# One of two graph product banks of the third slot is taken from the values: what a shift in a rotation of PSUM banks does

## Chip, cores, metric

One core of one Trainium2 chip. The metric is the device time of one execution in microseconds (us), median of several runs; each change is compared with runs of the kernel before on the same chip. Ratios are the mean time of one kernel's fast runs over that of the other's of the same rounds, so not quite the ratio of the medians quoted beside them. All runs told here were of the fast state. Names in the profile: PE is the TensorE's matmul, PEld its weight load, DVE the VectorE, ACT the ScalarE, POOL the GpSimd, SP the SyncE, which issues transfers. PSUM is the memory in which the kernel keeps PE's products, in banks.

## The reference, cut to what matters

64 graphs of 256 nodes with 512 features, fp32. A graph layer, then attention with 8 heads over the same mask, each with a residual and a layer norm:

```python
x = layernorm(x + gnn(x, adj, W, b))          # deg*(x Wi' + b) + A x Wj'
q, k, v = x Wq' + bq, x Wk' + bk, x Wv' + bv   # 8 heads of 64
out = softmax(mask(q k' / 8)) v
x = layernorm(x + out Wo' + bo)
```

## The kernel before

The kernel works on pairs of graphs; in one loop body it finishes the attention of one pair and does the graph layer of the next. Its matrix products are cut into seven block products (a Strassen scheme), whose left operands are sums of blocks. In the profile each fp32 matmul of the program stands as two pieces (a product of four matmuls is a row of x8); the graph products, whose operands are cast to fp32r, stand as one each, four to a product.

The kernel shares out eight banks of PSUM. Two score tiles hold two banks each, the values of the attention have one, and three go round among everything else:

```python
ps_s = ...(name="ps_s", bufs=2, space=PSUM)   # scores: 2 x 2 banks
ps_v = ...(name="ps_v", bufs=1, space=PSUM)   # values: 1 bank
ps_m = ...(name="ps_m", bufs=3, space=PSUM)   # all other products: 3 banks

def bank(name):
    return ps_m.tile([P, 512], F32, tag="mm", name=name)

def score_banks(name):
    return ps_s.tile([P, 2, 512], F32, tag="sc", name=name)
```

The graph stage makes, for each quarter c of the features, one product in a bank (`pa`), which ACT copies out and DVE reads in four sums:

```python
def take_input(b, c, pa):
    nc.scalar.copy(xl[b][:, c]..., pa[:, :3 * P])
    ...
    nc.vector.tensor_add(f["S1"][:, c], a21, f["A22"][:, c])
    nc.vector.tensor_sub(f["S3"][:, c], f["A11"][:, c], a21)
    nc.vector.tensor_sub(f["S2"][:, c], a22, f["S3"][:, c])
    nc.vector.tensor_sub(f["S4"][:, c], a12, f["S2"][:, c])   # last reader of the bank

def l0_inputs(b, half, borrow=False):
    ...
    for c in (2 * half, 2 * half + 1):
        pa = score_banks("pa")[:, 0, :] if borrow else bank("pa")
        ...                                                   # four matmuls
        take_input(b, c, pa)
```

The order of the work in a loop body (four slots between the products of the attention; b1, b2 are the graphs of the next pair, p and q their seven graph layer products, o the seven of the output projection):

```python
return [[item(l0_inputs, b1, 0, True), item(l0_inputs, b1, 1)],
        p[0:3] + [item(split_x, b2)] + p[3:4],
        p[4:7] + [item(l0_inputs, b2, 0)],
        [item(l0_inputs, b2, 1), q[0], q[1], item(h_transpose, b1, 1, True),   # third slot
         q[2], item(h_transpose, b1, 0, True)],
        q[3:], ...]
...
# fourth slot
run(o[:1] + rest[:1] + o[1:2] + rest[1:2])
combine_left(oS[g], in_order)
end_values(inverses)
run(rest[2:] + o[2:5] + work[SLOTS + 1] + o[5:6] + work[SLOTS + 2] + o[6:])
```

In the third slot pa2 and pa3 stand for the two graph products of `l0_inputs(b2, 1)`, x for product q[0] (it reads A11), w for q[1] (A22), A12 for q[2], which adds to x. In the profile `po` is the bank of such a product, `pav` that of the values, `den` that of the softmax sums.

Of the kernel before, what the change touches and what calls it, by code (L numbers as in the profile page):

```python
# [8 lines left out]
F32 = mybir.dt.float32  # L9
# [7 lines left out]
P = 128  # L17
# [208 lines left out]
def unshifted_path(ctx, tc, flag, x, adj, wiT, wjT, b0, wqT, bq, wkT, bk, wvT, bv, woT, bo, out):  # L226
# [14 lines left out]
    B, N, D = x.shape  # L241
# [21 lines left out]
    ps_v = ctx.enter_context(tc.tile_pool(name="ps_v", bufs=1, space=PSUM))  # L263
    ps_m = ctx.enter_context(tc.tile_pool(name="ps_m", bufs=3, space=PSUM))

    def bank(name):
        return ps_m.tile([P, 512], F32, tag="mm", name=name)

    def score_banks(name):
        return ps_s.tile([P, 2, 512], F32, tag="sc", name=name)  # L270


    def in_order(ins):

        tc.keep_in_program_order(ins)
# [4 lines left out]
    def matmul(*args, **kw):  # L280
        in_order(nc.tensor.matmul(*args, **kw))  # L281
# [194 lines left out]
    def input_tiles(b):  # L476
        xl[b] = p2.tile([P, NC, 3, P], F32, tag="xl", name="xl")
        a11, a12, a22 = (xl[b][:, :, m, :] for m in range(3))
        xS[b] = left_blocks(a11, a12, None, a22, p2.tile([P, 4, NC, P], F32, tag="xS", name="xS"))

    def graph_product(b, c, pa, n, t, part):
        matmul(pa[:, t * P:(t + 3) * P], part[:, t, c * P:(c + 1) * P], graph[:, t, :],
               start=(n == 0), stop=(n == 2 * NT - 1), skip_group_check=True)

    def take_input(b, c, pa):
        nc.scalar.copy(xl[b][:, c].rearrange("p m n -> p (m n)"), pa[:, :3 * P])
        _, a12, a22, a21 = (pa[:, m * P:(m + 1) * P] for m in range(4))
        f = xS[b]
        nc.vector.tensor_add(f["S1"][:, c], a21, f["A22"][:, c])
        nc.vector.tensor_sub(f["S3"][:, c], f["A11"][:, c], a21)  # L490
        nc.vector.tensor_sub(f["S2"][:, c], a22, f["S3"][:, c])
        nc.vector.tensor_sub(f["S4"][:, c], a12, f["S2"][:, c])  # L492

    def l0_inputs(b, half, borrow=False):


        if half == 0:
            input_tiles(b)
        for c in (2 * half, 2 * half + 1):
            pa = score_banks("pa")[:, 0, :] if borrow else bank("pa")  # L500
            for n, (t, part) in enumerate((t, part) for t in range(NT) for part in (xhi[b], xlo[b])):
                graph_product(b, c, pa, n, t, part)
            take_input(b, c, pa)
# [12 lines left out]
    def l0_steps(b):  # L516
        banks = {}

        def product(name, lname, n, first):
            if first:  # L520
                banks[name] = bank("po")[:, :H]
            for c in range(NC):
                matmul(banks[name], xS[b][lname][:, c, :], w0[:, n, c, :], start=(first and c == 0),
                                 stop=(c == NC - 1), skip_group_check=True)

        def place(t, j):
            return xh[b][:, t, j * H:(j + 1) * H]

        def add_to(dst, src):
            nc.vector.tensor_add(dst, src, dst)  # L530

        def step1():
            product("x", "A11", B11, True)
            u1 = p2.tile([P, H], F32, tag="lu", name="u1")
            nc.scalar.copy(u1, banks["x"])

            rest = xh[b].rearrange("p t (j o) -> p (t j) o", j=2)[:, 1:]
            nc.gpsimd.tensor_tensor(rest, rest, u1.unsqueeze(1).to_broadcast([P, 3, H]), ALU.add)  # L538

        def step2():  # L540
            product("w", "A22", T4, True)
            add_to(place(1, 0), banks["w"])

        def step3():
            product("x", "A12", B21, False)
            add_to(place(0, 0), banks["x"])

        def step4():
            product("y", "S2", T2, True)
            add_to(place(0, 1), banks["y"])  # L550

        def step5():
            product("z", "S1", T1, True)
            add_to(place(1, 1), banks["z"])

        def step6():
            product("y", "S3", T3, False)
            h = xh[b][:, 1, :].rearrange("p (j o) -> p j o", j=2)
            add_to(h, banks["y"].unsqueeze(1).to_broadcast([P, 2, H]))
            norm(xh[b][:, 1, :])  # L560

        def step7():
            product("z", "S4", B22, False)
            add_to(place(0, 1), banks["z"])
            norm(xh[b][:, 0, :])

        return [step1, step2, step3, step4, step5, step6, step7]
# [19 lines left out]
    def pair_blocks(m, tag):  # L587

        s = p1.tile([P, 4, 2, N], F32, tag=tag, name=tag)
        return left_blocks(m[:, 0:2, 0:N], m[:, 2:4, 0:N], m[:, 0:2, N:2 * N], m[:, 2:4, N:2 * N], s)  # L590
# [60 lines left out]
    def qk_steps(g, store, tag, bias, diff):  # L651

        def new_store():
            store[g] = p1.tile([P, NC, NB * N], F32, tag=tag, name=tag)

        def place(i, j):
            return store[g][:, 2 * j:2 * j + 2, i * N:(i + 1) * N]

        def biased(b):
            def evict(dst, ps):  # L660
                for m in range(2):
                    nc.scalar.activation(dst[:, m, :], ps[:, m, :], AF.Identity, bias=b[:, m:m + 1], scale=1.0)
            return evict

        def last(dst, ps, addend):
            for m in range(2):
                nc.vector.scalar_tensor_tensor(dst[:, m, :], ps[:, m, :], diff[:, m:m + 1],  # L667
                                               addend[:, m, :], ALU.add, ALU.add)

        return qkv_steps(g, True, new_store, place, biased(bias), biased(diff), last)  # L670
# [98 lines left out]
    pavs = {}  # L769
# [7 lines left out]
    def values(g, w):  # L777
        i, pr = divmod(w, NC)
        if w == 0:
            aoT[g] = p1.tile([P, NC, NB * N], F32, tag="aoT", name="aoT")  # L780
            oS[g] = pair_blocks(aoT[g], "oS")
        pp = w % 2
        if pp == 0:
            pavs[g] = ps_v.tile([P, 2, N], F32, tag="av", name="pav")
        pe, _ = made[g, w]
        for kc in range(NT):
            for j in range(2):
                h0 = (2 * pr + j) * DH
                matmul(pavs[g][j * DH:(j + 1) * DH, pp, :], vv[g][:, i, kc, h0:h0 + DH], pe[:, j, kc, :],
                       start=(kc == 0), stop=(kc == NT - 1))  # L790
# [55 lines left out]
    def layer0(g):  # L846

        b1, b2 = NB * g, NB * g + 1

        def item(f, *args):  # L850
            return lambda: f(*args)

        p, q = l0_steps(b1), l0_steps(b2)
        return [[item(l0_inputs, b1, 0, True), item(l0_inputs, b1, 1)],
                p[0:3] + [item(split_x, b2)] + p[3:4],
                p[4:7] + [item(l0_inputs, b2, 0)],
                [item(l0_inputs, b2, 1), q[0], q[1], item(h_transpose, b1, 1, True),
                 q[2], item(h_transpose, b1, 0, True)],
                q[3:],
                [item(h_transpose, b2, 1, True)], [item(h_transpose, b2, 0, True)]]  # L860

    def run(steps):
        for s in steps:
            s()
# [17 lines left out]
    p, q = l0_steps(0), l0_steps(1)  # L882
# [3 lines left out]
    bias_steps()  # L886
    make_factors(wqT, "wq", raw_q)
    run(p[5:])
    l0_inputs(1, 0, True)
    l0_inputs(1, 1)  # L890
    make_factors(wkT, "wk", raw_k)
    for _ in range(AHEAD):
# [7 lines left out]
    q = qk_steps(0, qT, "qT", bq_sb, bqd)  # L900
# [18 lines left out]
    for g in range(NG - 1):  # L919
        load_x(NB * (g + 2))  # L920
        load_x(NB * (g + 2) + 1)
        work = layer0(g + 1)
        run(work[0])
        for w in range(2, NB * NC, 2):
            values(g, w - 2)
            values(g, w - 1)
            multiply()
            divide_two(g, w - 1)
            later = [scores(g, w), scores(g, w + 1)]
            part = work[w // 2]  # L930
            n = 0 if w == NB * NC - 2 else 1
            run(later[:n] + part[:1] + later[n:] + part[1:])
        w = NB * NC - 2
        values(g, w)
        values(g, w + 1)
        multiply()
# [8 lines left out]
        q = qk_steps(g + 1, qT, "qT", bq_sb, bqd)  # L945
# [10 lines left out]
    g = NG - 1  # L956
# [89 lines left out]
```

## Time and profile before

| | before |
|---|---|
| median of the first 3 runs | 3230.88 us (3230.29 to 3233.19) |
| PE busy | 3189.2 us, 99% of the span |
| next engine, DVE | 59% |
| granted PE clock | 0.998 |
| one period of the loop | 99.68 us, 31 of them |

How to read it: PE is the bound, by its busy share, but "busy" has modelled ends in it: pieces that start 216 ns apart are drawn 380 ns long. What PE loses is read from the distance between starts of matmuls, as the prediction does. The period is taken from the first graph product of one loop body to that of the next; 31 bodies give 30 such distances.

### The profile page before, as it was taken

Reading aid. Unit: us, or ns where it says so; the run is one execution under the profiler, and the core shown is the slowest. Engines: PE = TensorE matmul, PEld = TensorE weight load, DVE = VectorE, ACT = ScalarE, POOL = GpSimd, SP = SyncE. Lnnn points to the kernel's source line nnn. Section 1 sums busy time; section 2 is a strip of 40 time slices with the busy share of each in tenths; the row PEclk is TensorE's granted clock in tenths of the full one; section 3 lists DMA queues with packets and bytes.
Section 4 is the critical chain, followed back from the end, with each engine's and each line's share of the span. In section 5 each row is a group of like instructions: output and inputs, shape, how many; then the busy total and the mean of one; then the engine's idle time right before and its main releaser. Section 6 shows DMA issues by size and latency. Waiting matters only on the chain. (4 is left out here: it accounts for less than half of the span.)

```text
span 3230.8 us, 48219 instructions
## 1 busy us (share of the span) xinstructions
PE 3189.2 (99%) x17398; PEld 2617.4 (81%) x17398; DVE 1892.0 (59%) x3847; ACT 1113.0 (34%) x2146; POOL 1506.9 (47%) x1191
## 2 busy tenths in 40 slices
PE   8999999999999999999999999999999999999998
PEld 6888888888888888888888888888888888888885
DVE  6655556555565555655556655556555565555665
ACT  2333333333333333333333333333333333333333
POOL 3454444544445444455444454344544445444443
PEclk9999999999999999999999999999999999999999
DMA  7234432344323433223443234432334322444223
GB/s 246 64 107 122 121 97 74 102 118 123 112 66 92 120 121 118 74 87 111 123 123 90 74 106 121 121 106 67 99 119 123 113 69 90 118 121 119 80 70 92
DMA packets 257168, 340.90 MB, mean 106 GB/s; under 512 B 29856, under 2 KB 154272, under 8 KB 256928
## 3 DMA queue, kind: packets, MB, share of 16 engines
q1 hardware_dynamic: 256928, 337.76, 34.9%
q8 instruction: 143, 2.34, 0.3%
q14 instruction: 97, 0.79, 0.1%
HBM read 274.73 MB, written 37.75 MB: 97 GB/s over the span
## 5 line engine op out<-in xcount | busy, mean ns | idle before, releaser
L454 POOL TENSOR_TENSOR rstd<-ve,mhalf 128x1 f32<-128x1 f32 x256 | 140.6, 549 | 813.6 <-DVE below L452 813.0
L281 PE MATMUL po<-w,xS 128*128 128x256 f32 x2048 | 474.9, 382 | 4.4 <-DVE xh L530 0.5
L281 PE MATMUL st<-hS,factor 128*128 128x256 f32 x2048 | 454.4, 380 | 2.5 <-DVE u L636 2.5
L763 POOL TENSOR_TENSOR pk<-pe 128x512 f32<-128x512 f32 x256 | 322.1, 1274 | 276.9 <-ACT pe L760 276.9
L281 PEld LDWEIGHTS po<-w,xS 128*128 128x128 f32 x2048 | 384.4, 190 | 77.4 <-DVE xh L530 17.2
L281 PEld LDWEIGHTS st<-hS,factor 128*128 128x128 f32 x2048 | 390.2, 191 | 56.3 <-DVE u L636 2.9
L281 PE MATMUL po<-w,xl 128*128 128x256 f32 x1536 | 360.1, 384 | 16.8 <-DVE xS L492 15.9
L760 ACT ACTIVATE pe<-pe 128x1024 f32<-128x1024 f32 x256 | 270.2, 1057 | 248.2 <-DVE pe L756 248.2
L281 PEld LDWEIGHTS po<-w,xl 128*128 128x128 f32 x1536 | 284.0, 190 | 73.3 <-PE po L281 22.9
L281 PE MATMUL st<-hT,factor 128*128 128x256 f32 x1536 | 342.2, 379 | 1.0 <-DVE qT L667 1.0
L636 DVE TENSOR_TENSOR u<-st,u 128x512 f32<-128x512 f32 x96 | 66.4, 692 | 468.8 <-PE st L281 461.6
L756 DVE TENSOR_TENSOR pe<-ps,maskT 128x1024 f32<-128x1024 f32 x256 | 297.1, 1201 | 67.6 <-PE ps L281 67.6
L530 DVE TENSOR_TENSOR xh<-po,xh 128x256 f32<-128x256 f32 (+1 forms) x384 | 170.5, 458 | 268.2 <-POOL xh L538 197.1
L281 PEld LDWEIGHTS st<-hT,factor 128*128 128x128 f32 x1536 | 291.7, 190 | 40.9 <-DVE qT L667 1.4
L281 PE MATMUL ps<-qT,kT 64*128 64x256 f32 x2048 | 256.5, 389 | 0.0
L281 PE MATMUL pav<-pe,v_sb 128*64 128x256 f32 x2048 | 250.1, 386 | 1.9 <-ACT pe L760 1.8
L281 PEld LDWEIGHTS ps<-qT,kT 64*128 64x128 f32 x2048 | 187.0, 186 | 68.2 <-issue 51.3
L281 PE MATMUL st<-factor,hS 128*128 128x256 f32 x1024 | 234.8, 382 | 0.0
L281 PE MATMUL st<-factor,oS 128*128 128x256 f32 x992 | 229.4, 379 | 0.0
L833 DVE RECIPROCAL rden<-den 128x256 f32<-128x256 f32 x96 | 168.8, 1758 | 91.6 <-PE den L281 86.1
L281 PEld LDWEIGHTS st<-factor,hS 128*128 128x128 f32 x1024 | 191.9, 190 | 35.4 <-issue 10.6
L459 ACT ACTIVATE shift<-below,rstd 128x1 f32<-128x1 f32 x256 | 75.4, 294 | 415.2 <-POOL rstd L454 409.6
(112 smaller groups left out, 5035.9 us busy)
## 6 DMA issues: line engine op xcount, KB each, us to landing
xh<-in_x_dram SPq DMA_DIRECT2D x64, 512.0 KB, 4.0
factor<-wq SPq DMA_DIRECT2D x128, 256.0 KB, 2.7
factor<-wk SPq DMA_DIRECT2D x128, 256.0 KB, 2.6
factor<-wv SPq DMA_DIRECT2D x128, 256.0 KB, 4.3
factor<-wo SPq DMA_DIRECT2D x124, 256.0 KB, 2.7
out_dram<-xh SPq DMA_DIRECT2D x62, 512.0 KB, 4.1
factor<-in_wqT_dram SPq DMA_DIRECT2D x96, 256.0 KB, 2.7
factor<-in_wkT_dram SPq DMA_DIRECT2D x96, 256.0 KB, 2.7
```

The source lines that it names most:

```text
L281: in_order(nc.tensor.matmul(*args, **kw))
L454: nc.gpsimd.tensor_tensor(rstd, ve, mhalf, ALU.pow)
L459: order(nc.scalar.activation(shift, below, AF.Identity, scale=rstd))
L530: nc.vector.tensor_add(dst, src, dst)
L636: nc.vector.tensor_add(new("u2"), bank["y"], k["u1"])
L756: nc.vector.tensor_add(pe.rearrange("p j t q -> p j (t q)"), ps.rearrange("p j t q -> p j (t q)"), maskT.rearrange("p t q -> p (t q)").uns ...
L760: in_order(nc.scalar.activation(flat, flat, AF.Exp, scale=QSCALE, accum_out=etot[:, NB * g + i, pr:pr + 1]))
L763: nc.gpsimd.tensor_tensor(pk, pe[:, :, 0, :], pe[:, :, 1, :], ALU.add)
L833: nc.vector.reciprocal(rden, den)
```

## The change

Intent: in the third slot the first graph product goes to the bank of the values, which is free there, so that one tile fewer goes round the three banks and w gets the bank of another, earlier tile.

```diff
+    def score_bank(name):
+        return score_banks(name)[:, 0, :]
+
+    def value_bank(name):
+        return ps_v.tile([P, 512], F32, tag="av", name=name)
...
-    def l0_inputs(b, half, borrow=False):
+    def l0_inputs(b, half, borrow=()):
...
-            pa = score_banks("pa")[:, 0, :] if borrow else bank("pa")
+            pa = borrow[c % 2]("pa") if borrow else bank("pa")
...
-            pavs[g] = ps_v.tile([P, 2, N], F32, tag="av", name="pav")
+            pavs[g] = value_bank("pav").rearrange("p (r q) -> p r q", r=2)
...
-        return [[item(l0_inputs, b1, 0, True), item(l0_inputs, b1, 1)],
+        return [[item(l0_inputs, b1, 0, (score_bank, score_bank)), item(l0_inputs, b1, 1)],
...
-                [item(l0_inputs, b2, 1), q[0], q[1], item(h_transpose, b1, 1, True),
+                [item(l0_inputs, b2, 1, (value_bank, bank)), q[0], q[1], item(h_transpose, b1, 1, True),
```

(One more call, ahead of the loop, gets its argument in the new form.)

## The prediction

> **What bounds the kernel now.** I read the page's head first, then the waits of PE, then one period of the loop in order of time, on PE and on the engines that free its banks.

> ```profile
> span 3230.8 us, 48219 instructions
> PE 3189.2 (99%) x17398; PEld 2617.4 (81%) x17398; DVE 1892.0 (59%) x3847; ACT 1113.0 (34%) x2146; POOL 1506.9 (47%) x1191
> PEclk9999999999999999999999999999999999999999
> ```

> PE is busy 3189.2 of 3230.8 us at a full clock, no other engine over 59%. So the end is set by PE, and a change that neither removes matmuls nor makes them shorter can win at most PE's lost time. The program has 17398 matmuls before and after; what order each engine gets is the same too (I compared the built programs: only waits differ). The waits of PE say where it is lost:

> ```profile
> PE po L281 <- DVE xS L492: 15.9, 32, 4.5
> PE pt_a L284 <- DVE a L324: 4.1, 1, 4.1
> PE st L281 <- DVE u L636: 2.5, 1, 2.5
> PE pa L281 <- ACT xhi L368: 2.2, 1, 2.2
> ```

> Columns: total us, times, longest. Only the first line recurs: 32 times, of which one of 4.5 us (the start of the program; its other lines are single waits too) and 31 short ones, (15.9 - 4.5) / 31 = 0.37 us each. 31 is the number of times that the loop body with the graph stage runs (32 pairs of graphs, the first one's stage stands ahead of the loop). One period on PE, third slot, from the timeline (start, us, engine, line, operation, tiles, count):

> ```profile
> 1024.76 0.44 PE L281 MATMUL pa<-graph,xhi 128*128 128x384 f32 x1
> ...
> 1026.10 0.34 PE L281 MATMUL pa<-graph,xlo 128*128 128x384 f32 x1
> 1026.27 1.89 PE L281 MATMUL po<-w,xl 128*128 128x256 f32 x8
> 1028.51 1.97 PE L281 MATMUL po<-w,xl 128*128 128x256 f32 x8 [0.35 <-DVE xS L492]
> 1030.32 0.60 PE L284 MATMUL pt_h<-ident,xh 128*128 128x128 f32 x4
> 1030.75 1.89 PE L281 MATMUL po<-w,xl 128*128 128x256 f32 x8
> 1032.48 0.60 PE L284 MATMUL pt_h<-ident,xh 128*128 128x128 f32 x4
> 1033.01 1.95 PE L281 MATMUL pav<-pe,v_sb 128*64 128x256 f32 x16
> ```

> The reader is to see starts, not durations: eight pieces that run unhindered take 32.48 - 30.75 = 1.73 us from their start to the next start (216 ns each, though each is drawn 380 long). The first eight (product x) took 28.51 - 26.27 = 2.24, and the eight after the wait (product w) 30.32 - 28.51 = 1.81, since the first interval after a standstill is longer. Lost: 0.51 + 0.08 = 0.59 us. What it waited for, on DVE:

> ```profile
> 1022.38 0.28 DVE L492 TENSOR_TENSOR xS<-pa,xS 128x128 f32<-128x128 f32 x1
> 1022.58 0.28 DVE L491 TENSOR_TENSOR xS<-pa,xS 128x128 f32<-128x128 f32 x1
> 1022.89 0.29 DVE L492 TENSOR_TENSOR xS<-pa,xS 128x128 f32<-128x128 f32 x1
> 1023.29 1.76 DVE L833 RECIPROCAL rden<-den 128x256 f32<-128x256 f32 x1
> 1024.96 2.29 DVE L756 TENSOR_TENSOR pe<-ps,maskT 128x1024 f32<-128x1024 f32 x2
> 1027.17 0.28 DVE L489 TENSOR_TENSOR xS<-pa,xl 128x128 f32<-128x128 f32 x1
> ...
> 1028.09 0.28 DVE L492 TENSOR_TENSOR xS<-pa,xS 128x128 f32<-128x128 f32 x1
> ```

> and on ACT:

> ```profile
> 1022.67 0.56 ACT L800 COPY aoT<-pav 128x512 f32<-128x512 f32 x1
> ...
> 1028.94 0.36 ACT L535 COPY u<-po 128x256 f32<-128x256 f32 x1
> ```

> The four sums that read the first graph bank stand on DVE behind a reciprocal of 1.76 and two mask additions of together 2.29 us; the last ends at 1028.09 + 0.28 = 1028.37, and w starts 0.14 later. w's data had been there long before.

> [...]w (256 columns of a bank) must wait for the last reader of whatever stood there; the trace agrees (0.14 us after it). [...]in the trace the transposes after w, with data and bank ready, wait too. [...]starts 216 ns apart, durations of 380; hence an idle of 0.35 where 0.59 is lost.

> **The change, part by part.** The three product banks go round: a tile gets the bank of the third tile before it. In the third slot the order was den, pa2, pa3, x, w, then den, x, y, z of the fourth slot, after z, pa0, pa1 of the second. Now pa2 goes to the bank of the values and drops out of the round. (At the other two call sites the argument only changes form: score banks before and after. The value tile has the same size and bank.) Work, sizes and transfers: nothing added, nothing removed. Only these bank waits move, each with what is left of it by the timeline above (start of the waiter less end of the reader):
> - pa2: from pa0's readers to ACT's copy of the values: 1024.76 - 1023.23 = 1.5 us to spare.
> - pa3: from pa1's to pa0's readers: start some 1025.5, reader done 1022.66: 2.8 to spare.
> - x: from the reciprocal to pa1's readers: 1026.27 - 1023.18 = 3.1 to spare.
> - w: from pa2's readers (late by 0.51) to the reciprocal, done at 1025.05. w could start at 1026.27 + 1.73 = 1028.00: 2.9 to spare. This is the wait removed.
> - values of slots 6, 7: now behind pa2's readers, 1028.37, for a start of 1033.01 - 0.59 = 1032.42: 4.0 to spare.
> - den and the products of the fourth slot keep the predecessors that they had.

> Sum: 31 periods x 0.59 = 18.3 us. One of the 31 (the one that starts at 1094 us, where the timeline has x at 1125.94 and w at 1128.54, so 2.60 for 2.24) waits 0.36 longer: 18.65 in all. All of it is on the path, as PE is the path. 3230.88 - 18.65 = 3212.2 us, a ratio of 1.006.

> **The rivals.**
> First: what is won is lost again at the next wait behind it. Candidates, with PE 0.59 earlier: product A12 adds to x's bank after ACT's copy of it (done 1028.94 + 0.36 = 1029.30; A12 would start at 1030.16: 0.86 left, the tightest); the two transposes behind the mask additions (done by 1027.25, start 1029.73). They all hold. There is a second lost interval in each period, which the weight loads show better than PE:

> ```profile
> PEld po L281 <- DVE xh L530: 17.2, 32, 0.9
> 1035.87 1.76 DVE L814 RECIPROCAL rden<-den 128x256 f32<-128x256 f32 x1 [2.74 <-PE den L281]
> 1041.04 5.73 PE L281 MATMUL po<-w,xS 128*128 128x256 f32 x24
> 1046.61 1.89 PE L281 MATMUL st<-factor,aoT 128*128 128x256 f32 x8
> ```

> 24 pieces took 46.61 - 41.04 = 5.57 where 24 x 0.216 = 5.18 would do: 0.39 lost to a DVE addition. If what holds that addition did not move, the 0.59 would be added there and the change would win nothing (3231). Against: the DVE chain to it starts with a reciprocal for which DVE idles 2.74 us until PE's den; den comes 0.59 earlier, and the chain with it. I expect this loss to stay at 0.39, neither cured nor grown. If half the gain went there: 3222.

> Second: the value bank is the bottleneck, as there is one alone: pa2 waits for ACT. For it: ACT copies late if its queue is full (the copy came 0.34 us after the values' end). Against: 1.5 us to spare, and periods alike (first graph product to first graph product 99.67 to 99.69 us, one of 100.03). If ACT came 2 us later in each period the loss would be 0.5 x 31 = 15 us and cancel the gain: 3228.

> Third: more than 0.59, if the second loss were cured as well: 31 x 0.39 = 12 us more, 3200. Nothing in the change touches the bank or the reader there.

> **Range and chances.** The measured runs before spread over 3230.29 to 3233.19, so 3 us; the gain's own error is small, as the period repeats to 0.02 us. I predict 3212.3 us, 3209 to 3218 eight times in ten; the upper side is wider for a part of the gain given back. Two per cent would be 64.6 us: all of PE's idle time is 3230.8 - 3189.2 = 41.6, so faster by 2% is as good as excluded (0.005); slower by 2% would need 2.1 us in each period against spare times of 0.86 and more (0.005); within 2%: 0.99.

> **What would show it.** Right: the recurring wait of PE for the sums of line L492 (moved by six lines) falls from 32 to 1 and from 15.9 to some 4.5 us; x, w and the first transpose of the third slot start 1.73 us apart; the period falls from 99.68 to 99.09; the weight loads' wait for the addition into xh stays near 17. Wrong: a recurring wait of pa for the ACT copy of the values, of the values for the sums, or a larger interval in the fourth slot. A clock under full would void the sum.

## The result, and the profile after

3214.42 us, median of 6 runs (3213.57 to 3215.25), against 3231.64 us for 6 runs of before; ratio 0.9946, 95% interval 0.9933 to 0.9959. That is within 2%, and 2.1 us over the predicted 3212.3.

The head of the page after; line numbers are six higher from here on:

```profile
span 3213.5 us, 48157 instructions
PE 3180.5 (99%) x17398; PEld 2625.5 (82%) x17398; DVE 1892.0 (59%) x3847; ACT 1111.8 (35%) x2146; POOL 1505.4 (47%) x1191
```

Same matmuls, 62 instructions fewer: two wait instructions of PE in each of 31 periods. The first lines of PE's waits (total us, times, longest):

```profile
PE po L287 <- DVE xS L498: 7.2, 1, 7.2
PE pt_a L290 <- DVE a L330: 4.2, 1, 4.2
PE pa L287 <- ACT xhi L374: 2.2, 1, 2.2
```

The wait for the four sums, 32 times before, is there once, at the start of the program. (Its 7.2 us instead of the 4.5 that the prediction named belong to the start; in the repetition below it is 2.1.) And the third slot in order of time:

```profile
1021.88 3.62 PE L287 MATMUL po<-w,xl 128*128 128x256 f32 x16
1025.34 0.60 PE L290 MATMUL pt_h<-ident,xh 128*128 128x128 f32 x4
1025.77 1.89 PE L287 MATMUL po<-w,xl 128*128 128x256 f32 x8
1027.50 0.60 PE L290 MATMUL pt_h<-ident,xh 128*128 128x128 f32 x4
```

x and w are now one row of 16 pieces without a pause: 1025.34 - 1021.88 = 3.46 us, where before 1030.32 - 1026.27 = 4.05 went by. The period is 99.08 us, all 30 of them between 99.07 and 99.09. The fourth slot kept its loss:

```profile
1036.06 5.73 PE L287 MATMUL po<-w,xS 128*128 128x256 f32 x24
1041.63 0.59 PE L287 MATMUL st<-factor,aoT 128*128 128x256 f32 x2
```

Its 24 pieces still take 1041.63 - 1036.06 = 5.57 us.

To see where the rest went I cut each trace in three: the start up to the first graph product of the loop, the 31 periods, the end. (No graph product closes the last period; it is taken as long as the median one.)

| trace | start | loop | end | span |
|---|---|---|---|---|
| before | 97.55 | 3090.32 | 42.95 | 3230.82 |
| after | 98.53 | 3071.56 | 43.38 | 3213.47 |
| difference | -0.98 | 18.76 | -0.43 | 17.35 |

The loop won 18.76 us against a predicted 18.65. Start and end gave 1.4 of it back. Whether that is chance or a price is one question of the experiments; the other is whether it was the bank at all.

### The profile page after: what moved, and what is told of

Read it like the earlier page. It is cut to its first block, busy times and chain, and to the rows that moved or that the text cites. A ratio compares the mean times of both kernels' runs of the same rounds, so it can differ in the third digit from the quotient of the medians.

```text
span 3213.5 us, 48157 instructions
## 1 busy us (share of the span) xinstructions
PE 3180.5 (99%) x17398; PEld 2625.5 (82%) x17398; DVE 1892.0 (59%) x3847; ACT 1111.8 (35%) x2146; POOL 1505.4 (47%) x1191
## 5 line engine op out<-in xcount | busy, mean ns | idle before, releaser
L287 PEld LDWEIGHTS po<-w,xS 128*128 128x128 f32 x2048 | 385.4, 191 | 76.3 <-DVE xh L536 17.3
L287 PE MATMUL po<-w,xl 128*128 128x256 f32 x1536 | 353.3, 383 | 8.1 <-DVE xS L498 7.2
```

Of the source, the lines that this page charges most:

```text
L287: in_order(nc.tensor.matmul(*args, **kw))
```

## The experiments

Theory: w found its bank occupied at a moment that DVE sets, 0.51 us too late, and PE lost 0.59 us with the restart; anything that lets the bank be free by then, or fills the time, wins the same. Rivals: the gain comes from fewer wait instructions on PE; from the values' bank as such; or it comes back at a later wait.

**The changed kernel once more** (no edit).

> The changed kernel once more, to part the loop from the start and the end of the program. In the first trace of it the loop won 18.8 us, the start lost 1.0 and the end 0.7 against before, 17.35 in all. If start and end are chance (the order in which transfers land), this run's start and end differ from those by up to some us while the loop's period is again 99.08; time 3212 to 3216. If they are a price of the change, start and end come out as in the first trace, within 0.2 us.

3210.88 us (5 runs; before 3230.96; ratio 0.9942), 1.1 us below the range that I gave. Period 99.08, loop 3071.62. The start was 93.58 us, 4.95 shorter than in the first trace: chance. The end was 43.46, as in the first: not chance, it seemed (see the last but one experiment). By the table above the first trace's end had lost 0.43 us, not the 0.7 of the expectation. The next three experiments ran on the same chip as this one, so this is the changed kernel that they are to be compared with.

**The second bank instead of the first.**

```diff
-[item(l0_inputs, b2, 1, (value_bank, bank)), q[0], ...
+[item(l0_inputs, b2, 1, (bank, value_bank)), q[0], ...
```

> The second of the two graph banks goes to the bank of the values instead of the first. Theory (what counts is that one of the two leaves the round of three, so that w no longer gets the bank of pa2): same time as the changed kernel, 3214.4 within 1 us, period 99.08, no recurring wait of w. Rival (what counts is which bank the first graph product gets, or the value bank is itself a faster place): w waits for pa2 as before, 3231.

3213.23 us (5 runs, ratio 0.9948), period 99.085, PE's wait for the sums again only once. Which of the two leaves the round does not matter; that one leaves it does. The time is 1.2 us under the first result, 0.2 more than I had allowed, and 2.4 over the repetition; in the two traces 1.3 of that is the start (94.91 against 93.58).

**Before, one transpose ahead of w**, no change of banks.

```diff
-[item(l0_inputs, b2, 1), q[0], q[1], item(h_transpose, b1, 1, True),
- q[2], item(h_transpose, b1, 0, True)],
+[item(l0_inputs, b2, 1), q[0], item(h_transpose, b1, 1, True), q[1],
+ q[2], item(h_transpose, b1, 0, True)],
```

> Before, with its bank round as it was, but the first transpose of h moved ahead of w. Theory (the loss is only that w's bank comes free at a fixed time, 0.51 us too late for PE): the transpose fills 0.44 us of it, 0.07 to 0.15 us are left per period, gain 14 us, 3217 to 3219. Rival (the gain of the change is from two wait instructions fewer per period on PE, not from time waited for DVE): both wait instructions are still there, so 3231.

3216.16 us (5 runs, ratio 0.9956): 14.8 less than before, 0.8 under the range that I gave. The period is the surer number: 99.23, so 0.15 of the 0.59 was left, its upper end. In the trace (x, the transpose, then w and A12 together):

```profile
1018.47 1.89 PE L281 MATMUL po<-w,xl 128*128 128x256 f32 x8
1020.20 0.60 PE L284 MATMUL pt_h<-ident,xh 128*128 128x128 f32 x4
1020.72 3.69 PE L281 MATMUL po<-w,xl 128*128 128x256 f32 x16
```

w starts 1020.72 - 1020.20 = 0.52 us after the transpose instead of the 0.43 that the four pieces need (1030.75 - 1030.32 in the trace of before): it still waits a little, for the same bank: 0.09 here, and from w to the second transpose 3.52 us go by (1024.24 - 1020.72) where the changed kernel needs 3.46, which makes the 0.15.

**Before, both transposes ahead of w.**

```diff
+[item(l0_inputs, b2, 1), q[0], item(h_transpose, b1, 1, True),
+ item(h_transpose, b1, 0, True), q[1], q[2]],
```

> Before, with both transposes of h ahead of w, bank round as it was. Theory: 0.87 us of other work stand before w, its bank is free by then, and the whole 0.59 per period is gone: 3213 to 3215, as fast as the changed kernel, period 99.08 to 99.10. Rival (wait instructions): 3231. Rival (the loss comes back at the next wait when PE is early): more than 3218.

3210.68 us (5 runs, ratio 0.9939), period 99.085: the whole gain without any change of banks, as fast as the changed kernel on the same chip (3210.88). This kernel has as many wait instructions on PE as before (48219 instructions in both pages), so the rival of the instructions falls. The time is 2.3 us below the range that I gave, probably since the start of this trace (93.77 us) is 4.8 us shorter than the one that I had reckoned from (98.53).

**Both graph products in the one bank of the values**, a late bank on purpose.

```diff
-[item(l0_inputs, b2, 1, (value_bank, bank)), q[0], ...
+[item(l0_inputs, b2, 1, (value_bank, value_bank)), q[0], ...
```

> Both graph products of the third slot go to the one bank of the values. Theory (a late bank is paid in full by PE): the second graph product waits for the four sums of the first, from 1025.5 to some 1028.5 on the clock of the first trace, 3.0 us per period, 31 x 3.0 = 93 us over the changed kernel: 3300 to 3312. Rival (the idle is hidden because other engines catch up): under 3260.

3347.84 us (4 runs, ratio 1.0364): 36 us above the range. The wait itself came out as expected. PE's first wait and the place in the timeline (pa2 ends, pa3 waits, then x and w):

```profile
PE pa L287 <- DVE xS L498: 84.5, 31, 3.1
```

```profile
1056.94 0.34 PE L287 MATMUL pa<-graph,xlo 128*128 128x384 f32 x1
1059.99 0.66 PE L287 MATMUL pa<-graph,xhi 128*128 128x384 f32 x1 [2.72 <-DVE xS L498]
...
1061.41 5.88 PE L287 MATMUL po<-w,xl 128*128 128x256 f32 x16
1067.13 0.60 PE L290 MATMUL pt_h<-ident,xh 128*128 128x128 f32 x4
```

What I had not reckoned with is the last step: x and w take 1067.13 - 1061.41 = 5.72 us where 3.46 are needed. The clock tells why; the same trace by windows (length, busy us of the engines with instructions, granted PE clock, DMA share, GB/s):

```profile
1057.50:1064.00 6.50, 4.01 (x11) 3.50 (x12) 3.34 (x10) 2.64 (x5) 0.75 (x1) 0.63 0.16 40
1064.00:1068.00 4.00, 4.00 (x18) 3.37 (x17) 0.42 (x1) 0.82 (x4) 4.00 (x4) 0.75 0.00 0
```

After 2.7 us of idle the PE clock was halved: 0.63 over 6.50 us and 0.75 over 4.00 are what one stretch of 6.83 us at half clock makes, and the graph pieces in it start 0.32 us apart (1061.09 - 1060.77) where 0.18 is usual (1056.94 - 1056.76). In this trace's loop 20 stretches at half clock stand, of 3.41 or 6.83 us; in the loops of before and after there is none. Not every gap brought one: after that of 2.71 us ahead of 1370.79 the graph pieces start 0.18 us apart. The periods without one are 102.01 to 102.03 us long: 99.08 + 2.95, the wait of 3.0 as worked out. The others are 103.65 to 105.02. Of the mean excess, 103.51 - 99.08 = 4.43 us over the 30 periods, the wait is 2.95 and the clock some 1.5. All the stretches in this trace begin on one grid of 3.413 us, the length of the shorter ones, which does not follow the periods. Laid on this grid, each of the 20 gaps that brought half clock left one step of it idle for at least 0.57 of its length, and none of the other 11 left more than 0.55 of any (idle counted from 0.18 us after the last start to the next start). So here where the gap falls on the grid decides whether a period is hit.

**A cure of the second loss**: the A22 product of the output projection moved ahead of the last graph layer product, in the changed kernel.

```diff
-run(rest[2:] + o[2:5] + work[SLOTS + 1] + ...
+run(rest[2:3] + o[2:3] + rest[3:] + o[3:5] + work[SLOTS + 1] + ...
```

> The changed kernel, and the product of the output projection that needs A22 moved ahead of the last graph layer product in the fourth slot. Theory: the second loss of each period, 0.39 us before that product, is a wait for a DVE addition of fixed lateness; 1.73 us of other work hide it, and 31 x 0.39 = 12 us are gained: 3201 to 3204, period 98.69. Rival (DVE is the limit in this slot, behind two reciprocals of 1.76 us, and the wait only moves to the next product): 3212 to 3216.

3201.91 us (5 runs, ratio 0.9911), period 98.69. In the fourth slot (the two graph layer products, the A22 product between, the last one):

```profile
1032.52 3.62 PE L287 MATMUL po<-w,xS 128*128 128x256 f32 x16
1035.97 1.89 PE L287 MATMUL st<-factor,aoT 128*128 128x256 f32 x8
1037.70 1.89 PE L287 MATMUL po<-w,xS 128*128 128x256 f32 x8
1039.42 3.62 PE L287 MATMUL st<-factor,oS 128*128 128x256 f32 x16
```

32 pieces take 1039.42 - 1032.52 = 6.90 us, 216 ns each, no loss left.

**The same move in the kernel before.**

> The same move in the kernel before. Theory: the two losses are apart and add: 3231.6 less 12 = 3218 to 3221, the third slot still with its wait of 0.59. Rival (one chain on DVE feeds both waits, so curing one changes the other): gain under 8 or over 16 us.

3219.5 us (6 runs, ratio 0.9968), period 99.28, 0.40 less than before; PE's wait for the sums is still there 32 times with 16.2 us. The two losses are independent and add. (The move also takes away one wait instruction of PE per period, 31 in all; here, other than in the third slot, no run parts the two, and the loss is put down to the wait by the distances of starts alone.)

**The end of the program.** By now the ends of the traces had sorted themselves: 43.38, 43.46, 43.55 and 44.27 us in the kernels with one graph product in the values' bank (43.61 in the one with both, cut at the same instruction), 42.46, 42.46, 42.56 and 42.95 in those with the old round. The products of the last pair's attention, after the loop, are the same instructions in all of them. One softmax sum (`den`) starts there 0.6 to 1.0 us later, behind POOL, which waits with a multiplication for eight transfers of 32 KB that SyncE issues. In that moment of the changed kernel (a window of 1.5 us on the DMA queues: what moved, and the issues with KB and us to landing):

```profile
q8 instruction: 1, 0.02, 4.8%
issues: line engine op xcount, KB each, median us to landing
spread<-rden SPq DMA_DIRECT2D x2, 32.0 KB, 2.5
```

A fetch of instructions, one 16 KB packet, runs while the second transfer is issued; that issue takes 1.31 us where its neighbours take 0.58. The changed kernel has 62 instructions fewer on PE, so, I supposed, the fetches of PE's program fall on other moments. The test puts them back:

```diff
-run([p[0], p[2], p[1]])
+run([p[0], p[2]])
+spare = value_bank("spare")
+for _ in range(16):
+    matmul(spare[:, :1], ident, ones[:, :1], start=True, stop=True)
+run([p[1]])
```

> The changed kernel with 16 one-column matmuls (64 instructions on PE) put into a stretch near the start where PE waits for DVE anyway. The four traces of kernels with the changed bank have the end of the program 0.6 to 1.0 us longer than the four with the bank round of before, and in one of them a 16 KB packet of the instruction queue runs while SyncE issues the second of eight small transfers that the first multiplication after the loop waits for. Theory (PE has 62 instructions less, so its instruction fetches fall on other moments, and one now falls on those transfers): with 64 instructions more the fetch is back where it was, at some 5.8 us ahead instead of 2.4, and the end is 42.4 to 43.0 us long; loop 3071.6 as in the changed kernel. Rival (the bank of the values itself makes the end longer): 43.3 to 43.6. Time 3210 to 3215 in both, too close to tell by time alone.

3211.65 us (5 runs, ratio 0.9942), loop 3071.58. The fetch moved to 5.7 us ahead of the same matmul (5.8 in before, 2.4 in after) and the end shrank to 42.70 us. The same window of this trace:

```profile
DMA packets 0, 0.00 MB, mean 0 GB/s; under 512 B 0, under 2 KB 0, under 8 KB 0
...
spread<-rden SPq DMA_DIRECT2D x2, 32.0 KB, 1.8
```

and the multiplication on POOL, in the changed kernel and then in this one (the bracket is POOL's idle ahead of it):

```profile
3183.25 1.27 POOL L801 TENSOR_TENSOR aoT<-aoT,spread 128x512 f32<-128x512 f32 x1 [0.90 <-DVE pe L762]
```

```profile
3178.95 1.27 POOL L801 TENSOR_TENSOR aoT<-aoT,spread 128x512 f32<-128x512 f32 x1 [0.17 <-issue]
```

The profile names DVE as the releaser in the first line: a mask addition that ended at 3183.10. In before the multiplication starts (3200.30) ahead of the end of that addition (3200.88), so that addition is not what it waits for; by the trace the multiplication starts 0.33 us after the landing of the last of its eight transfers in before, in the changed kernel, in its repetition and in this one alike, so the transfers set it. In the changed kernel with the A22 product moved the packet falls on the seventh transfer itself, which lands 3.1 us after its issue began instead of 1.9. In the two kernels of the old round with that move, which have 31 instructions fewer than before, the packet moved too, but to a moment ahead of the eight transfers, and nothing was lost. So the values' bank is not at fault; padding alone cures it. (Of the end of 44.27 us this explains 0.8; some 0.9 more lie after the start of the last projection product, which stands 9.7 us from the end there and 8.7 to 9.1 in the other ten traces; that stays open.) No mark on the packet says that the fetch is PE's own, but the counts do: the pages have 143 packets on its queue, q8 (2.34 MB in before, so 16 KB each), in the three kernels with 36084 instructions of PE (before, and the two with only transposes moved) and in the padded one (36086), and 142 in the seven with 36053 or fewer; the other engines' instructions are the same in all eleven.

**Order alone**: the old bank round, both transposes ahead of w and the A22 product moved.

> The bank round of before, with both transposes ahead of w and the A22 product ahead of the last graph layer product. Theory: both recurring losses are hidden by order alone, no bank of the values needed: period 98.69 as in the kernel with the changed bank and the same move, loop 3059.5, time 3198 to 3203, equal to that kernel's 3201.9 within the chance of the start. Rival (transposes ahead of w make something later wait when the fourth slot is tight): more than 3206.

3200.24 us (4 runs, ratio 0.9906), period 98.69, loop 3059.53. It is as fast as the changed kernel with the same move, and needs no borrowed bank. It has the lowest median of all, 0.9% under before; the 2% mark of the verdict it does not reach either.

## Why the prediction was right, point by point

- **PE is the bound, and its lost time is the most there is to win.** Right: what PE's loop lost the time lost too, to within the chance of start and end, and the other engines' busy times hardly changed (DVE 1892.0 us in both, ACT 1113.0 and 1111.8, POOL 1506.9 and 1505.4). But the 41.6 us that the prediction calls all of PE's idle time is no upper limit, by its own argument: 17.35 us went out of the span while that idle fell by 8.6 only (3213.5 - 3180.5 = 33.0 after); the rest had been hidden in "busy". Nothing hung on it.
- **0.59 us per period, not the 0.37 that the waits add up to.** Right: the period fell by 0.59. The sum of the waits (31 x 0.37 = 11.4 us) would have been 7 us too low, for modelled ends hide a part (0.35 us drawn as idle in the prediction's timeline, where the starts lie 0.51 us further apart than usual), and the slow first interval after a standstill (0.29 us instead of 0.216) is in no wait at all.
- **The new waits have time to spare.** Right: none of the waits listed with 1.5 to 4.0 us to spare appears in the waits after. A12 behind ACT's copy kept 0.86 us.
- **First rival, the second loss of 0.39 grows.** It did not: 5.57 us for its 24 pieces before and after. Its DVE chain hangs on PE's den and moved with it: the reciprocal that opens it starts 9.01 us after x (1030.89 - 1021.88) instead of 9.60 (1035.87 - 1026.27). Nor was it cured, as the third rival had it: the weight loads' wait for that addition stayed, 17.2 before and 17.3 after. The two experiments with the A22 product show that it was separate, and worth 12 us.
- **Second rival, the values' bank comes late.** It did not with one product in it. With two it did, and cost 2.95 us of wait per period.
- **The sum.** 18.65 us predicted, 18.76 in the loop. The term that was mis-sized is the one that I set to nothing: "nothing added, nothing removed" outside the loop. The end cost 0.4 us in this pair of traces and some 0.9 by the means (first three changed ends 43.46, four old ones 42.6), because fewer instructions on PE move the instruction fetches (62 fewer brought one from 5.8 to 2.4 us ahead of the same matmul). The start, 93.6 to 98.5 us in the eleven traces, does not go with the kind of kernel, and varies by more than that; it is the likely reason why the changed kernel measured 3214.42 in one set and 3210.88 in another, with one trace of each set to show it. The four starts of 97.5 us and more have 6.8 to 10.2 us of half PE clock in them, the seven others 3.4. What decides that was not pursued. That the first result came out only 2.1 us from the predicted time is in part luck of the start: the repetition of the same kernel was 1.4 us on the other side.

## What to carry to other kernels

Where PE sets the end, look in the order of time for starts of matmuls that lie further apart than the steady interval, and take the loss from those distances (here 216 ns was steady, 732 went by over the wait and 291 right after it); a wait that shows as 0.37 us was worth 0.59. A tile that comes too early for its bank can be helped from two sides with the same result: give one tile of the round another bank (3210.88 us here), or put other ready work ahead of it (3210.68 us on the same chip). Before borrowing a bank, write down for each new pair of tile and predecessor how long the reader will have been done; with two tiles in one borrowed bank the kernel ended 117 us slower than before, six times what the borrowing of one had won.
